# Moving the transposes of q and of the attention output off TensorE, in a linear attention followed by a sparse feed-forward layer

## The chip, the cores and the metric

The kernel runs on one core of a Trainium2 chip. The metric is the time of one execution on the device, in microseconds (us); the time before is the median of three runs.

## What is computed

The input x has 2 batches of 1024 tokens with 512 features, in float32. Two layers follow each other, each with a normalized input and a normalized, added output:

```
x = x + layernorm(attention(layernorm(x)))
x = x + layernorm(ffn(layernorm(x)))

attention: q = x Wq^T (16 heads of 128), k = x Wk^T, v = x Wv^T (4 heads of 128, each used by 4 heads of q)
           q, k = rope(q), rope(k);  qf, kf = elu(q) + 1, elu(k) + 1
           per token: state += kf v^T;  z += kf;  out = (qf . state) / (qf . z + 1e-6)
           attention = out Wo^T
ffn:       h = silu(x Wgate) * (x Wup)    (2048 wide)
           of every 4 neighbours in h keep the 2 of largest magnitude;  ffn = h Wdown
```

## The kernel before

**Tiles.** Attention runs in 16 steps: first all eight chunks of 128 tokens (both batches at once) with the first half of the heads, then the eight chunks again with the second half (`STEPS = 2 * NC`). In a step there are four blocks, one for each pair of batch and k/v head (`GROUPS`); a block has 128 tokens of four q heads that share one k head. The scan over tokens is done by chunk: scores of a block against its own chunk, masked to the causal half, plus the state of the chunks before.

**Products.** Each projection is a Strassen product in seven parts (`strassen`, L109): seven products of half-sized sums of inputs and weights, in the order 1, 2, 6, 5, 7, 4, 3, added into one PSUM bank `cb`, with copies to SBUF (`keep`, L120, ScalarE) in between and final sums on VectorE (L129, L139, L145). The sums of weights for the first half of the heads are built in SBUF by `sums`; those for the second half, and for the feed-forward layer, by a background generator `preparing`, of which one unit is a load on SP, four sums on GpSimd and seven stores on SP; it is advanced once for each block.

**q.** `q_products` (L634) gives four blocks; each goes through `features` (L584): the rotation (VectorE, L592 to L599; an addition on GpSimd, L600), ELU + 1 (two ScalarE activations, L602 and L603, and a VectorE operation, L604). The result `qf` has tokens on partitions. `q_transposed` (L663) turns it with four 128x128 TensorE transposes into PSUM (`transposed`, L528, L532), and ScalarE copies it to `qT` (L665), with head features on partitions and, for each head, 128 tokens in a row.

**Scores and numerators.** `scores` (L668) multiplies k's transposed block with all four heads of `qT`; VectorE masks the result into `am` (L679). `attend` (L684) takes for each head h the 128 tokens of `qT` and `am` as the stationary operand, against state and v, and VectorE divides by the denominator (L703 to L706). The quotient `o` has tokens on partitions, one head after the other.

**The output projection.** `o_transposed` (L733) turns `o` in the same way; the blocks are the inputs of `o_products` (L747), the fourth after subtractions (L741 to L745). A step's output projection runs in the next step.

**Order.** TensorE, GpSimd and SP follow the order in which the program is written (`manual_schedule`); VectorE and ScalarE are ordered by a planner, but for a short part at the start. SP issues nearly all transfers, and its issues wait in order. In step n the loop writes: `first(0)` (transposes of q block 1 and of the last step's output block 3), five of k/v's products for step n + 1, `second(0)` (numerators of block 0, scores of block 1), the rest of k/v, q's products for step n + 1 with block 1 in between, k's transposes, then the output products of step n - 1 around blocks 2 and 3. The last step interleaves the first gate products of the feed-forward layer.

**Buffers.** PSUM: three banks for products (`ps_mm`), two for transposes (`ps_tr`), one for scores, two for numerators. x has three buffers, `qf` three, `qT` two.

Of the kernel before, what the change touches and what calls it, by code (L numbers as in the profile page):

```python
# [15 lines left out]
P = 128  # L16
# [19 lines left out]
def kernel(  # L36
# [21 lines left out]

    ident = const.tile([P, P], F32, name="ident")
# [13 lines left out]
    eps = const.tile([P, 1], F32, name="eps")  # L73
    nc.gpsimd.memset(eps, LN_EPS)
# [12 lines left out]
    xf_dram = [dram.tile([P, 7, 2, P], F32, name=f"xf{c}") for c in range(NC)]  # L87
    y_dram = [dram.tile([P, B, DM], F32, name=f"y{c}") for c in range(NC)]
# [5 lines left out]
    def layernorm_scale(src, tag):  # L94

        st = small.tile([P, nc.vector.BN_STATS_DIM], F32, tag=f"st{tag}", name="st")
        nc.vector.bn_stats(st, src)
        mv = small.tile([P, nc.vector.BN_AGGR_DIM], F32, tag=f"mv{tag}", name="mv")
        nc.vector.bn_aggr(mv, st)
        sd = small.tile([P, 1], F32, tag=f"sd{tag}", name="sd")  # L100
        nc.scalar.activation(sd, mv[:, 1:2], AF.Sqrt, bias=eps)
        rs = small.tile([P, 1], F32, tag=f"rs{tag}", name="rs")
        nc.vector.reciprocal(rs, sd)
        return mv[:, 0:1], rs
# [4 lines left out]
    def strassen(pools, shape, product, c11, c12, c22, done):  # L109
# [24 lines left out]
        e = bank("ce")  # L134
# [4 lines left out]
        nc.vector.tensor_tensor(c22, s3, e, ALU.add)  # L139
# [5 lines left out]
        nc.vector.tensor_tensor(c12, s2, e, ALU.add)  # L145
# [42 lines left out]
    def ffn_input(xns, psum, tag, engine=None):  # L188
        xnT = pool["xs"].tile([P, NIC, 4 * P], F32, tag="fxnT", name="fxnT")
        for tt in range(4):  # L190
            pt = psum.tile([P, NIC, P], F32, tag=tag, name="psx")
            for j in range(NIC):
                nc.tensor.transpose(pt[:, j, :], xns[tt][:, j, :], ident)
            nc.scalar.copy(xnT[:, :, tt * P : (tt + 1) * P], pt)
        t = pool["xs"].tile([P, 3, 2, 256], F32, tag="fxt", name="fxt")
        return combinations(
            t,
            xnT[:, 0:2, 0:256],
            xnT[:, 0:2, 256:512],
            xnT[:, 2:4, 0:256],  # L200
            xnT[:, 2:4, 256:512],
            engine,
        )
# [110 lines left out]
    def down(hf):  # L314


        def product(bank, i, start):
# [3 lines left out]
            for jb in range(NJB):  # L321
                for j in range(2):
                    for k in range(2):
                        nc.tensor.matmul(  # L324
                            bank[:, j, :],
                            hf[jb][hi][:, k, j * P : (j + 1) * P],
                            w[:, jb, k, :],
                            start=(start and jb == 0 and j == 0 and k == 0),
                            stop=(jb == NJB - 1 and j == 1 and k == 1),
                            skip_group_check=True,  # L330
                        )
# [10 lines left out]
                lambda t: nc.scalar.copy(y[:, 0:2, 256:512], t),  # L342
            )
# [3 lines left out]
    def ffn_output(m, tt, xt_, y):  # L347
        b, c = place(m, tt)
        mean, rs = layernorm_scale(y, "y")
        yn = pool["ln"].tile([P, DM], F32, tag="ln", name="fyn")  # L350
        normalize(yn, y, mean, rs)
        nc.gpsimd.tensor_tensor(yn, xt_, yn, ALU.add)  # L352
# [22 lines left out]
    xp = left("a_x", 3)  # L375
# [4 lines left out]
    ps_mm = left("ps_mm", 3, space=PSUM)  # L380
    ps_tr = left("ps_tr", 2, space=PSUM)
# [30 lines left out]
    def sums(t, engine):  # L412
        a11, a12, a22, s2, s4, s3, s1 = (t[:, i] for i in range(7))
        for o, i0, i1, op in (
            (s1, s3, a22, ALU.add),
            (s3, a11, s3, ALU.subtract),
            (s2, s1, a11, ALU.subtract),
# [9 lines left out]
    xt = {0: load_x(0)}  # L427
# [3 lines left out]
    load_quarters(wq_sb, q_quarter, (nc.scalar, nc.sync))  # L431
    rope_sb = rawp.tile([P, NC, 3, HD // 2], F32, name="rope_sb", bufs=1)
    nc.scalar.dma_start(out=rope_sb, in_=rope.rearrange("(c p) t d -> p c t d", p=P))
    xt[1] = load_x(1)
    wo_sb = new_factors("wo", 4, 256)
    load_quarters(wo_sb, o_quarter, (nc.sync,))
    xt[2] = load_x(2)
# [96 lines left out]

    xf = {}
# [9 lines left out]
    def step_input(n, xns):  # L545

        t = ln.tile([P, 7, 2, P], F32, tag="xf", name="xf")
        xf[n] = t
        for b in range(B):
# [6 lines left out]
        nc.vector.tensor_tensor(t[:, 4], t[:, 2], t[:, 3], ALU.subtract)  # L556
        nc.vector.tensor_tensor(t[:, 5], t[:, 4], t[:, 0], ALU.subtract)
        nc.vector.tensor_tensor(t[:, 6], t[:, 1], t[:, 4], ALU.subtract)
        nc.sync.dma_start(out=xf_dram[n], in_=t)
# [24 lines left out]
    def features(src, c, dst):  # L584

        half = HD // 2
        cos = rope_sb[:, c, 0, :].unsqueeze(1).broadcast_to([P, 8, half])
        nsin = rope_sb[:, c, 1, :].unsqueeze(1).broadcast_to([P, 4, half])
        psin = rope_sb[:, c, 2, :].unsqueeze(1).broadcast_to([P, 4, half])
# [8 lines left out]
        nc.vector.tensor_tensor(r[:, :, 0:half], src[:, :, half:HD], nsin, ALU.mult)  # L598
        nc.vector.tensor_tensor(r[:, :, half:HD], src[:, :, 0:half], psin, ALU.mult)  # L599
# [8 lines left out]
    kf, kT, v1, qf = {}, {}, {}, {}  # L608
    GROUPS = ((0, 0), (1, 1), (0, 1), (1, 0))

    def kv_products(n):
        c = n % NC
# [13 lines left out]
        features(raw, c, f)  # L626
# [7 lines left out]
    def q_products(n):  # L634
        c = n % NC
        raw = [rawp.tile([P, REP, HD], F32, tag="raw", name="qraw", bufs=4) for _ in range(3)]

        def feature(i, src):
            f = qp.tile([P, REP, HD], F32, tag="qf", name="qf", bufs=3)
            features(src, c, f)  # L640
            qf[n, i] = f
# [19 lines left out]
    qT, am, o = {}, {}, {}  # L661

    def q_transposed(n, i):  # L663
        t = qp.tile([P, REP, P], F32, tag="qT", name="qT")
        nc.scalar.copy(t, transposed(qf.pop((n, i))))  # L665
        qT[n, i] = t

    def scores(n, i):  # L668
        b, j = GROUPS[i]
        sc = ps_sc.tile([P, REP, P], F32, tag="sc", name="sc")  # L670
        nc.tensor.matmul(  # L671
            sc.rearrange("p h t -> p (h t)"),
            kT[n][:, 2 * b + j, :],
            qT[n, i].rearrange("p h t -> p (h t)"),
# [3 lines left out]
        t = qp.tile([P, REP, P], F32, tag="am", name="am")  # L678
        nc.vector.tensor_tensor(  # L679
            t, sc, causal.unsqueeze(1).broadcast_to([P, REP, P]), ALU.mult  # L680
        )
        am[n, i] = t

    def attend(n, i):  # L684
# [8 lines left out]
        q, a = qT.pop((n, i)), am.pop((n, i))  # L693
        for h in range(REP):
            dst = nmv[:, h // 2, h % 2, :]
            if c > 0:
                nc.tensor.matmul(dst, q[:, h, :], state[b, j], start=True, stop=False)  # L697
            nc.tensor.matmul(dst, a[:, h, :], v, start=(c == 0), stop=True)  # L698
# [6 lines left out]
        t = qp.tile([P, REP, HD], F32, tag="o", name="o")  # L705
# [6 lines left out]
        o[n, i] = t  # L712
# [12 lines left out]
    later = []  # L725
# [6 lines left out]

    def o_transposed(n, i):  # L733

        t = transposed(o.pop((n, i)))
        if i < 3:
            place = (0, 2, 1)[i]
            nc.scalar.copy(factor(n, place, 1 if place == 1 else 2), t)
        else:
            t1, t2, t3, t4 = (factor(n, 3 + k, 1) for k in range(4))  # L740
            nc.vector.tensor_tensor(t1, t, of[n, 0], ALU.subtract)  # L741
            nc.vector.tensor_tensor(t2, of[n, 2], t1, ALU.subtract)
            t3_engine = nc.gpsimd if n + 1 < STEPS else nc.vector
            t3_engine.tensor_tensor(t3, t2, of[n, 0], ALU.subtract)
# [265 lines left out]
```

## Time and profile before

| | |
|---|---|
| median of 3 runs | 1395.71 us (1395.39 to 1396.8) |
| the profiled execution | 1395.51 us |
| its span, first to last instruction | 1393.8 us |
| TensorE busy / weight loads busy | 1335.9 / 1069.0 us |
| VectorE / ScalarE / GpSimd busy | 835.1 / 447.3 / 321.5 us |
| bytes moved by DMA | 197.48 MB, mean 142 GB/s |

A line of the profile's groups names line, engine, operation, output <- inputs, shapes and count, then busy time and the mean of one in nanoseconds. Busy times on TensorE overlap between neighbours, since matmuls are pipelined; the distance from start to start is what one holds of the engine. A wait line has waiter <- releaser, then total us, times, longest. L532 is line 532 of the kernel shown.

### The profile page before, as it was taken

How to read it: one execution, taken by the hardware profiler on the slowest of the kernel's cores; microseconds unless marked ns; L12 is line 12 of the kernel's file. 1: busy time of each engine (PE TensorE's matmuls, PEld its weight loads, DVE VectorE, ACT ScalarE, POOL GpSimd, SP SyncE). 2: the span in 40 equal slices, each digit the busy share in tenths (PEclk: the TensorE clock that was granted, in tenths of full speed). 3: DMA queues.
4: the chain of work that ended last, by engine and by line, in shares of the span. 5: the costliest groups of instructions: out<-in, count | busy, mean ns of one | idle time of the engine just before them, and what ended most of it. 6: DMA issues, size and time to landing. Idle time of an engine off the chain costs nothing. (4 is left out here: it accounts for less than half of the span.)

```text
span 1393.8 us, 17195 instructions
## 1 busy us (share of the span) xinstructions
PE 1335.9 (96%) x6384; PEld 1069.0 (77%) x6384; DVE 835.1 (60%) x1570; ACT 447.3 (32%) x797; POOL 321.5 (23%) x259
## 2 busy tenths in 40 slices
PE   4899999999999999999999999999999999999997
PEld 2567778777876787667678888888888888888886
DVE  5785766564556565656566439816772577526852
ACT  1543433433233324333342323214330333113210
POOL 0333322332333343444332110100000100110001
PEclk9999999999999999999999999999999999999999
DMA  6131345035841736233443455346544655355321
GB/s 245 42 125 52 105 162 186 28 97 178 274 140 64 242 113 215 82 108 123 153 144 129 128 213 152 116 165 217 152 128 152 222 153 154 117 201 152 91 79 73
DMA packets 109732, 197.48 MB, mean 142 GB/s; under 512 B 8272, under 2 KB 51280, under 8 KB 105552
## 3 DMA queue, kind: packets, MB, share of 16 engines
q1 hardware_dynamic: 107520, 194.02, 43.1%
q10 hardware_dynamic: 2128, 2.36, 0.5%
q8 instruction: 51, 0.84, 0.2%
q14 instruction: 33, 0.27, 0.1%
HBM read 145.23 MB, written 51.12 MB: 141 GB/s over the span
## 5 line engine op out<-in xcount | busy, mean ns | idle before, releaser
L120 ACT COPY u<-cb 128x512 f32<-128x512 f32 (+1 forms) x252 | 126.1, 500 | 474.7 <-PE cb L218 183.1
L600 POOL TENSOR_TENSOR u<-u,r 128x512 f32<-128x512 f32 x80 | 101.8, 1273 | 300.9 <-DVE r L599 190.1
L570 PE MATMUL cb<-wq,xf 128*128 128x512 f32 x256 | 121.3, 596 | 7.0 <-ACT u L120 7.0
L755 PE MATMUL cb<-wo,of 128*128 128x256 f32 x512 | 121.2, 379 | 0.5 <-ACT u L120 0.5
L218 PE MATMUL cb<-fxt,wgu 128*128 128x256 f32 x512 | 117.8, 381 | 1.0 <-ACT u L120 1.0
L218 PE MATMUL cb<-fxnT,wgu 128*128 128x256 f32 x512 | 116.9, 379 | 0.0
L755 PEld LDWEIGHTS cb<-wo,of 128*128 128x128 f32 x512 | 95.9, 190 | 26.3 <-issue 11.9
L218 PEld LDWEIGHTS cb<-fxt,wgu 128*128 128x128 f32 x512 | 96.6, 190 | 16.4 <-ACT u L120 3.6
L218 PEld LDWEIGHTS cb<-fxnT,wgu 128*128 128x128 f32 x512 | 97.1, 190 | 13.8 <-issue 0.5
L604 DVE SCALAR_TENSOR_TENSOR qf<-u,r 128x512 f32<-128x512 f32 x64 | 65.4, 1021 | 66.3 <-ACT r L603 58.4
L168 POOL TENSOR_TENSOR h<-h 128x512 f32<-128x512 f32 x16 | 23.5, 1467 | 331.1 <-DVE ht L165 331.1
L602 ACT ACTIVATE r<-u 128x512 f32<-128x512 f32 x80 | 50.4, 631 | 153.9 <-POOL u L600 153.9
L139 DVE TENSOR_TENSOR y<-u,ce 128x256 f32<-128x256 f32 (+1 forms) x20 | 9.5, 474 | 146.8 <-ACT u L120 146.8
L698 PE MATMUL nm<-v,am 128*128 128x129 f32 x512 | 96.0, 277 | 1.5 <-DVE am L679 1.5
L570 PEld LDWEIGHTS cb<-wq,xf 128*128 128x128 f32 x256 | 46.6, 190 | 55.9 <-issue 40.7
L697 PE MATMUL nm<-state,qT 128*128 128x129 f32 x448 | 86.6, 275 | 0.0
L698 PEld LDWEIGHTS nm<-v,am 128*128 128x128 f32 x512 | 76.8, 194 | 3.4 <-issue 3.3
L697 PEld LDWEIGHTS nm<-state,qT 128*128 128x128 f32 x448 | 71.0, 191 | 7.7 <-issue 6.2
L570 PE MATMUL cb<-wkv,xf 128*128 128x256 f32 x256 | 67.8, 388 | 1.9 <-DVE xf L556 1.4
L671 PE MATMUL sc<-qT,kT 128*128 128x512 f32 x128 | 66.1, 598 | 0.0
L324 PE MATMUL cb<-wd,h 128*128 128x256 f32 x256 | 58.3, 381 | 4.0 <-DVE h L306 3.9
L755 PE MATMUL ce<-wo,of 128*128 128x256 f32 x256 | 60.5, 379 | 0.0
(151 smaller groups left out, 2571.6 us busy)
## 6 DMA issues: line engine op xcount, KB each, us to landing
wgu<-gs SPq DMA_DIRECT2D x112, 256.0 KB, 2.7
wgu<-us SPq DMA_DIRECT2D x112, 256.0 KB, 2.7
wd<-d_dram SPq DMA_DIRECT2D x28, 1024.0 KB, 4.8
xf<-xf SPq DMA_DIRECT2D x16, 896.0 KB, 5.1
x<-in_x_dram SPq DMA_DIRECT2D x16, 512.0 KB, 5.9
gs<-wraw SPq DMA_DIRECT2D x28, 256.0 KB, 3.5
us<-wraw SPq DMA_DIRECT2D x28, 256.0 KB, 3.5
d_dram<-wraw SPq DMA_DIRECT2D x28, 256.0 KB, 2.8
```

The costliest lines, as they stand in the source:

```text
L120: nc.scalar.copy(t, b)
L168: (engine or nc.gpsimd).tensor_tensor(b12, b22, b12, ALU.subtract)
L218: nc.tensor.matmul(bank[:, j, :], w[:, k, j, :], xf[xi][:, k, :], start=(start and j == 0 and k == 0), stop=(j == 1 and k == 1), skip_grou ...
L324: nc.tensor.matmul(bank[:, j, :], hf[jb][hi][:, k, j * P : (j + 1) * P], w[:, jb, k, :], start=(start and jb == 0 and j == 0 and k == 0), ...
L570: nc.tensor.matmul(bank.rearrange("p h d -> p (h d)"), x_[:, xi, k, :], w[:, wi, k, :], start=(start and k == 0), stop=(k == 1), skip_grou ...
L600: nc.gpsimd.tensor_tensor(u, u, r, ALU.add)
L602: nc.scalar.activation(r, u, AF.Relu, scale=-1.0)
L604: nc.vector.scalar_tensor_tensor(dst, u, 0.0, r, ALU.max, ALU.add)
L671: nc.tensor.matmul(sc.rearrange("p h t -> p (h t)"), kT[n][:, 2 * b + j, :], qT[n, i].rearrange("p h t -> p (h t)"), start=True, stop=True,)
L697: nc.tensor.matmul(dst, q[:, h, :], state[b, j], start=True, stop=False)
L698: nc.tensor.matmul(dst, a[:, h, :], v, start=(c == 0), stop=True)
L755: nc.tensor.matmul(bank.rearrange("p h d -> p (h d)"), of[n, xi][:, k, :], w[:, wi, k, :], start=(start and k == 0), stop=(k == 3), skip_g ...
```

## The change

In words:

- q features: VectorE transposes 32x32 blocks inside the tile (`turned`), SP stores the result to HBM in one transfer of 256 KB (`q_store`), and four transfers of 64 KB bring it back with the blocks in their places (`q_load`). In the loaded tile the free axis is four groups of 32 tokens, each with all four heads; numerators are made for 32 tokens of four heads at a time, and the mask is taken in that order.
- The output blocks take the same way (`o_store`, `o_load`) straight into the inputs of the output products; the subtractions stand together in `o_sums`. The last step keeps TensorE's transposes.
- Order in a step: q's products come first, k/v's behind numerators of block 0; k's transposes stand between output products. Loads of the second half's weights are spread over a step.
- The rope table is loaded for each step; rotation's two half-sized products become one. x has two buffers, `qf` one, `qT` four; product banks are four, transpose banks one.
- Start: x in two halves on two queues, weight sums on GpSimd, ScalarE's root used once ahead. End: the last down product has two banks, so that half of it is finished ahead; statistics of two halves are merged, the last addition is on VectorE.

```diff
+    def turned(src):
+        t = qp.tile([P, 4, 4, 32], F32, tag="blocks", name="blocks", bufs=4)
+        nc.vector.transpose(
+            out=t.rearrange("p b i r -> p i b r"),
+            in_=src.rearrange("p i (b d) -> p i b d", d=32),
+        )
+        return t
+
+    def store_blocks(t, to):
+        nc.sync.dma_start(out=to, in_=t.rearrange("p b i r -> p (b i r)"))
+
+    def load_blocks(t, of_):
+        for b in range(4):
+            nc.sync.dma_start(
+                out=t[b * 32 : (b + 1) * 32],
+                in_=of_.rearrange("(u d) (b e) -> b d u e", u=4, b=4)[b],
+            )
...
         def feature(i, src):
-            f = qp.tile([P, REP, HD], F32, tag="qf", name="qf", bufs=3)
-            features(src, c, f)
-            qf[n, i] = f
+            f = qp.tile([P, REP, HD], F32, tag="qf", name="qf", bufs=1)
+            features(src, n, f)
+            q_blocks[n, i] = turned(f)
...
-    def q_transposed(n, i):
-        t = qp.tile([P, REP, P], F32, tag="qT", name="qT")
-        nc.scalar.copy(t, transposed(qf.pop((n, i))))
-        qT[n, i] = t
+    def q_store(n, i):
+        store_blocks(q_blocks.pop((n, i)), qb_dram[n % 2][i])
+
+    def q_load(n, i):
+        t = qp.tile([P, 4, P], F32, tag="qT", name="qT", bufs=4)
+        load_blocks(t, qb_dram[n % 2][i])
+        qT[n, i] = t
...
-        for h in range(REP):
-            dst = nmv[:, h // 2, h % 2, :]
+        for u in range(4):
+            dst = nmv[:, u // 2, u % 2, :]
             if c > 0:
-                nc.tensor.matmul(dst, q[:, h, :], state[b, j], start=True, stop=False)
-            nc.tensor.matmul(dst, a[:, h, :], v, start=(c == 0), stop=True)
+                nc.tensor.matmul(dst, q[:, u, :], state[b, j], start=True, stop=False)
+            nc.tensor.matmul(dst, a[:, u, :], v, start=(c == 0), stop=True)
...
+        if n + 1 < STEPS:
+            blocks[n, i] = turned(t)
+        else:
+            o[n, i] = t
...
-        nc.vector.tensor_tensor(r[:, :, 0:half], src[:, :, half:HD], nsin, ALU.mult)
-        nc.vector.tensor_tensor(r[:, :, half:HD], src[:, :, 0:half], psin, ALU.mult)
+        nc.vector.tensor_tensor(
+            r.rearrange("p h (t d) -> p h t d", t=2),
+            src.rearrange("p h (t d) -> p h t d", t=2)[:, :, ::-1, :],
+            sin,
+            ALU.mult,
+        )
...
-    ps_mm = left("ps_mm", 3, space=PSUM)
-    ps_tr = left("ps_tr", 2, space=PSUM)
+    ps_mm = left("ps_mm", 4, space=PSUM)
+    ps_tr = left("ps_tr", 1, space=PSUM)
```

The order of a step in the changed kernel, for a step in the middle (one line for each call; `run(g, k)` makes k of the seven products of g):

```
first(0):  o_store(n-1, 3); q_load(n, 3); o_load(n-1, 3); preparing
run(q, 5)
second(0): q_store(n+1, 0); attend(n, 0); scores(n, 1)
first(1):  o_store(n, 0); q_load(n+1, 0); o_load(n, 0); preparing
run(q, 1); run(kv, 1); finish(q); run(kv, 4)
second(1): q_store(n+1, 1); q_store(n+1, 2); attend(n, 1); scores(n, 2)
first(2):  q_store(n+1, 3); o_store(n, 1); q_load(n+1, 1); o_load(n, 1); load_rope(n+2); preparing
finish(kv); o_sums(n-1); input of step n+2; run(o, 3)
second(2): attend(n, 2); scores(n, 3)
first(3):  o_store(n, 2); q_load(n+1, 2); o_load(n, 2); preparing
run(o, 1); k_transposed(n+1); run(o, 1)
second(3): attend(n, 3); scores(n+1, 0)
finish(o)
```

## The prediction

> **What bounds the kernel now.** I read the page's engine table and slices first, then the stretches of one step, then the timeline of TensorE inside a step, the table of waits, and last the timelines of start and end. The engine table and TensorE's slices:
>
> ```profile
> PE 1335.9 (96%) x6384; PEld 1069.0 (77%) x6384; DVE 835.1 (60%) x1570; ACT 447.3 (32%) x797; POOL 321.5 (23%) x259
> ...
> PE   4899999999999999999999999999999999999997
> ```
>
> TensorE is full in all slices but the first two and the last. The scores of block 0 mark the steps; the stretch table over one step from there to there has length, then busy time of PE, PEld, DVE, ACT, POOL, then clock, DMA share, GB/s:
>
> ```profile
> 551.00:597.46 46.46, 45.90 (x231) 34.48 (x230) 28.25 (x60) 17.49 (x33) 18.47 (x15) 1.00 0.39 130
> 597.46:645.82 48.36, 46.12 (x231) 34.39 (x230) 31.16 (x60) 17.52 (x33) 21.54 (x17) 1.00 0.36 131
> ```
>
> A step is TensorE's 46 us, and 2 us more where it waits; VectorE has 15 us to spare, the DMA engines 60%. So work taken off TensorE comes off the time until something else is late. What a transpose holds is not its busy time. TensorE's timeline:
>
> ```profile
> 568.54 0.60 PE L532 MATMUL pst<-ident,qf 128*128 128x128 f32 x4
> ...
> 568.98 0.60 PE L532 MATMUL pst<-ident,o 128*128 128x128 f32 x4
> ...
> 569.41 1.88 PE L570 MATMUL cb<-wq,xf 128*128 128x512 f32 x4
> ```
>
> The second column is 0.60, but the next group starts after 0.44 and 0.43. Four transposes cost **0.435 us**. The waits of TensorE that the change could touch, in total, times, longest:
>
> ```profile
> PE pst L532 <- DVE x L107: 16.9, 2, 8.7
> PE cb L570 <- ACT u L120: 7.5, 6, 2.0
> PE pst L532 <- ACT qT L665: 5.8, 20, 0.9
> ```
>
> The first is the start, where TensorE has no other work. The second is a copy that waits in ScalarE's order behind a feature map; the third is the evacuation of transposes.
>
> **Transposes off TensorE.** 64 of q and 60 of the output's 64 go (the last step keeps four): 124 x 0.435 = **53.9 us**. The busy column would give 38.5 + 38.5 x 60/64 = 74.6, which is too much, since neighbours overlap. With them goes the third wait, **5.8 us**. ScalarE loses 64 copies at 579 ns and 45 at 584, 63 us in all, but isn't the bound: nothing counted.
>
> **VectorE's new work.** 124 transposes of 128x512 f32. No row shows one. Below, the nearest by form (one input, SBUF to SBUF, same size) is the normalization of fxn at 580 ns; above, the fused last operation of a feature, 1021 ns, whose mean includes waits beside GpSimd. The Trainium skill's "VectorE: DVE Perf Modes", section "The three transpose paths", speaks against the change: it prices a 128x128 bf16 transpose at 311 ns on VectorE, 32x32 blocks only, and its rules send a 128x128 transpose to TensorE where PSUM will do. By it (an estimate: 311 plus 384 more columns at the 0.96 GHz it gives) one of ours is 711 ns; against TensorE's measured 435 that is a loss if the two engines' time were worth the same. It isn't here: one has no idle time and the other 35%. I take 0.70 us, nearest to the 671 ns row of the x normalization. Eight a step are 5.6 us. Each feature's two rotated products (415 + 416 ns) become one of full size (about 690), 0.14 x 5 = 0.7 us less. VectorE goes from 28.6 us (mean over 13 steps) to **33.5** of a step of about 43, 78%. Cover is thus thinner: at 1.02 it is 36 us. The first of the subtractions for the output (L741, 687) now reads SBUF, at 690 to 951 like its neighbours; inside that rounding.
>
> **What is late next.** The matmuls with the numerators wait for the masked scores. After the reorder the shortest distance is for block 3: one output product (1.72), k's transposes (0.44), another product (1.72), 3.9 us, against 5.2 before. In it VectorE does the former block's den, reciprocal, o, the new transpose and the state (0.15 + 0.18 + 0.69 + 0.70 + 0.28 = 2.0, the first 0.9 of it before the scores end) and the mask, 0.68: done 1.8 us after the scores if VectorE is free, 2 us of slack. One operation that is held beside GpSimd (the trace has 1.75) eats that. I charge 0.5 us a step, 14 steps, **+7 us**; bounds 0 and 35 (2.5 a step).
>
> **q first, k later.** k's products move behind q's first five and block 0. Their chain (last sum at 565.60, kf done at 572.5) takes 7 us; k's transposes now stand three output products, one block and another product behind, 9.7 us. Block 0's scores follow 4 us later against one copy at 575 ns. Nothing on the path. If k is 3 us late, TensorE waits those 3.
>
> **The way through HBM.** q block 0: feature chain 5 to 8.5 us (568.81 to 577.31 is the longest I saw), transpose 0.7, store, load. A 256 KB store lands in 2.0 us (the output's row), a 256 KB load in 2.7 (weights of gate). The loads are four of 64 KB. "DMA: Bandwidth & Descriptors", section "Rules for kernel authors", says that under 64 KB one pays mostly overhead[...]. Taken one behind the other, 32 loads a step would be 64 us, longer than the step, and the change a loss. The trace has the 112 gate loads at 320 ns on SP each, landing at 2.7, so transfers overlap and the issue counts: four loads 1.3 us. From q product 2 to the loaded block: 8.5 + 0.7 + 2.0 + 1.3 + 2.7 = 15 us, and it is wanted at the end of the step, 35 us on. The output goes out at one step and is summed in the middle of the next: over 15 us to spare for its last block. **0 us**, as long as SP keeps up.
>
> **SP's order** is fixed by hand, so a store that waits for VectorE holds all behind it: q's and o's loads, the preparation of weights, x. A step had about 15 issues (prepared weights 10.7, four others); it gets 8 stores, 32 loads and a rope table, 56. The 15 take about 9 us (store pieces of 512 bytes 0.84, of weights 0.44, loads 0.7); 41 x 0.32 = 13; waits for VectorE, by my laying out of the order, 7. Together 29 of 43 us. GpSimd's preparation waits for loads that now stand behind those, some 4 us later within a quarter of a step of slack (10 us).
>
> **DMA engines.** 4.2 MB a step more, at the 287 GB/s of a stretch in which only stores from 512-byte pieces run, 14.5 us, on 0.39 x 46.5 = 18: 76% of 43. Not the bound on average.
>
> **Start and end.** VectorE's timeline at the start:
>
> ```profile
> 8.51 0.69 DVE L97 BATCH_NORM_STATS2 st<-x 128x6 f32<-128x512 f32 x1
> 15.68 0.69 DVE L97 BATCH_NORM_STATS2 st<-x 128x6 f32<-128x512 f32 x1 [6.48 <-DMA x<-in_x_dram]
> ```
>
> Batch 1 of the first tile stands behind the statistics of the second tile's x. That load is issued after the first input now, so this 6.5 us can go; the root's table (1.28) is loaded ahead, and x in halves on two queues saves about 1. On GpSimd the first two of the kv sums take 2.5 us, beside normalization; wq's four, 2.6 each as for wo, end some 12 us after kv starts, before product 3 wants the last. From 0 (another operation waits for the same load) to 11; I take **9**. At the end, the last sum, two statistics, normalization twice and GpSimd's 1.26 stand between TensorE's end at 1384.4 and the last issue at 1390.7. Half-sized sums (0.42 for 0.69), statistics of one half only and VectorE's add (0.69) leave 3.2 of 6.2: **3 us**.
>
> **Sum.** 1393.8 - 53.9 - 5.8 - 9 - 3 + 7 = 1329.1 span; the profiled execution has 1.7 around its span, 1330.8, and stands 0.2 under the median shown: **1331**.
>
> **Rivals.**
> *VectorE's order becomes the bound* (22%): its transposes at 1 us or its waits beside GpSimd make TensorE wait 2.5 us in each of 14 steps, 35 instead of 7: **1359**. For it: 78% load in fixed order and the 2.00 us wait already there. Against: 1.8 us of work in 3.9 at the tightest place.
> *The start and the waits go better* (20%): no new waits, 11 us at the start, and the 7.5 us of waits for copies vanish with ScalarE's 63 us: 1331 - 7 - 2 - 7.5 = **1315**.
> *SP can't issue in time, slower than before* (8%): the loads back up as the 512-byte stores do, 0.84 a piece instead of 0.32. 56 issues and the waits: 9 + 41 x 0.84 + 7 = 50 us a step against 46.7 now. The step is then SP's: 14 x 3.7 = 52 us, less the 12 of start and end: **1436**. It loses from 47.6 us a step on, an issue of 0.77. Against: pieces of a 64 KB load are a quarter of a 256 KB store's.
> The forecast itself has the remaining 50%.
>
> **From these to the range.** Faster 0.91, the remainder slower save 0.01 for no change; 0.2% either way, 2.8 us, is about what this measurement can tell. The range runs from 1307 (the better case, with 8 us for the order of waits I can't see) to 1367 (the VectorE case, same margin); SP's case and a little at each end stay outside.
>
> **What would show it.** Right: TensorE's 128x128 groups from qf and o gone but for the last four, its busy time near 1260; steps of 42.5 to 43.5 us; VectorE transposes near 0.70; the first kv product near 10 us; TensorE's waits few and under a microsecond. Wrong: waits of the numerators for masked scores (L679) or of scores for loaded q in each step, SP's loads at over 0.7 us, transposes over 1 us, or the kv product at 18 us still.

## The result, and the profile after

The changed kernel takes 1433.4 us (median; 1429.74 to 1440.19) against 1395.72 us for the kernel before, run beside it: a ratio of 1.0274, 95% interval 1.0232 to 1.0316. It is slower by 38 us where 65 us less were forecast. The profiled execution took 1429.74 us, its span is 1428.0.

The page's engine table and TensorE's slices with the granted clock, after:

```profile
PE 1313.1 (92%) x5888; PEld 1033.9 (72%) x5888; DVE 892.0 (62%) x1612; ACT 402.1 (28%) x698; POOL 336.0 (24%) x265
...
PE   5889989899789878898898999999999999999997
...
PEclk9889999999989999999999999999999999999999
```

TensorE lost its 496 transposing matmuls (6384 to 5888), but its busy time fell by 22.8 us only, from 1335.9 to 1313.1, and what it is not busy rose from 57.9 us to 114.9. The slices, nines from the third on before, have eights and sevens up to slice 22, near the end of attention. Two stretches from one step's first scores to the next's, same columns as before:

```profile
580.28:627.20 46.92, 44.35 (x199) 32.49 (x198) 32.90 (x63) 13.89 (x26) 19.14 (x15) 0.96 0.62 196
627.20:678.20 51.00, 45.80 (x199) 32.84 (x198) 34.92 (x63) 14.11 (x26) 21.83 (x17) 0.93 0.71 234
```

With 32 matmuls less, TensorE is busy nearly as long as before (44.35 and 45.80 us against 45.90 and 46.12), at a clock of 0.96 and 0.93, and stands 2.6 and 5.2 us besides. The mean of the 14 steps is 49.6 us ((781.33 - 86.62) / 14, from the scores of step 1 to those of step 15), against 46.7 before. The new operations in the groups, and the transfers (count, size, median us from issue to landing):

```profile
L581 DVE STREAM_TRANSPOSE blocks<-qf 128x512 f32<-128x512 f32 x64 | 44.9, 702 | 0.3
...
L581 DVE STREAM_TRANSPOSE blocks<-o 128x512 f32<-128x512 f32 x60 | 41.4, 689 | 0.0
```

```profile
qT<-qb SPq DMA_DIRECT2D x256, 64.0 KB, 2.3
of<-ob SPq DMA_DIRECT2D x240, 64.0 KB, 2.0
```

A transpose costs what it was priced at, 0.70 us. The issue of a 64 KB load holds SP for 0.47 us in the mean of the 14 steps (median 0.43), where 0.32 was forecast. The waits of TensorE, after (total, times, longest):

```profile
PE cb L635 <- ACT u L133: 27.2, 23, 5.5
PE ce L635 <- DVE r L662: 14.3, 10, 2.8
...
PE pst L568 <- DVE kf L672: 8.7, 7, 4.3
PE cb L635 <- DMA xf<-xf: 8.3, 2, 7.3
PE cb L838 <- DVE of L825: 8.3, 4, 3.2
PE cb L635 <- DMA wq<-wq_dram: 7.9, 1, 7.9
```

None of these six was above 8 us before. A product waits for ScalarE's copy of the bank that it adds to, for VectorE's read of a bank (`r` is the rotation of q's third block, read from PSUM), for k's features, for the sums of loaded output blocks, and for loads. The waits that the prediction looked for, numerators for masked scores, are not among them.

What such a wait costs is more than its length. TensorE's timeline after, and three stretches behind waits (length, busy times, then clock, DMA share, GB/s):

```profile
395.69 3.75 PE L635 MATMUL cb<-wq,xf 128*128 128x512 f32 x4 [7.88 <-DMA wq<-wq_dram]
...
403.09 1.88 PE L635 MATMUL cb<-wq,xf 128*128 128x512 f32 x4
```

```profile
396.00:400.00 4.00, 4.00 (x8) 1.93 (x8) 0.00 (x0) 0.52 (x1) 0.00 (x0) 0.50 1.03 377
...
210.00:214.00 4.00, 4.00 (x11) 3.18 (x12) 4.00 (x9) 0.84 (x2) 0.00 (x0) 0.50 0.17 66
...
556.80:560.00 3.20, 3.20 (x11) 2.84 (x12) 2.80 (x4) 1.53 (x4) 1.26 (x1) 0.50 0.67 188
```

The four matmuls behind 7.88 us of waiting take 3.75 us at a clock of 0.50, the same four 1.88 us some 7 us later. The second stretch follows a wait of 5.48 us, the third two shorter ones, of 2.78 and 1.00 us within 5 us.

### The profile page after: what moved, and what is told of

It is laid out like the page before. It is cut to its first block, busy times and chain, and to the rows that moved or that the text cites. A ratio compares the mean times of both kernels' runs of the same rounds, so it can differ in the third digit from the quotient of the medians.

```text
span 1428.0 us, 17352 instructions
## 1 busy us (share of the span) xinstructions
PE 1313.1 (92%) x5888; PEld 1033.9 (72%) x5888; DVE 892.0 (62%) x1612; ACT 402.1 (28%) x698; POOL 336.0 (24%) x265
## 4 chain that ended last, share of the span: by engine, by line
PE 64%; DVE 16%; DMA 5%; ACT 5%; issue 4%; POOL 3%; SPq 3%; DVEq 0%; ACTq 0%; POOLq 0%
PE cb L237 15%; PE ce L237 8%; PE cb L346 6%; PE cb L838 6%; PE cb L635 5%; PE ca L237 4%; PE ce L346 4%; POOL u L668 3%; PE nm L766 3%; DVE blocks L581 2%; PE nm L765 2%; PE ce L838 2%; DVE r L662 2%; PE sc L740 2%; PE ce L635 2%
## 5 line engine op out<-in xcount | busy, mean ns | idle before, releaser
L668 POOL TENSOR_TENSOR u<-u,r 128x512 f32<-128x512 f32 x80 | 106.0, 1326 | 308.8 <-DVE r L662 240.4
L635 PE MATMUL cb<-wq,xf 128*128 128x512 f32 x256 | 128.5, 626 | 23.5 <-DMA xf<-xf 8.3
L838 PE MATMUL cb<-wo,of 128*128 128x256 f32 x512 | 124.9, 388 | 9.6 <-DVE of L825 8.3
L635 PEld LDWEIGHTS cb<-wq,xf 128*128 128x128 f32 x256 | 49.6, 199 | 83.8 <-issue 65.9
L766 PE MATMUL nm<-v,am 128*128 128x129 f32 x512 | 101.0, 289 | 2.1 <-ACT state L787 2.1
L765 PE MATMUL nm<-state,qT 128*128 128x129 f32 x448 | 92.1, 289 | 0.0
L635 PE MATMUL cb<-wkv,xf 128*128 128x256 f32 x256 | 73.4, 413 | 19.9 <-ACT u L133 19.9
L672 DVE SCALAR_TENSOR_TENSOR qf<-u,r 128x512 f32<-128x512 f32 x64 | 58.2, 910 | 48.4 <-ACT r L671 43.4
L766 PEld LDWEIGHTS nm<-v,am 128*128 128x128 f32 x512 | 82.4, 206 | 3.8 <-ACT state L787 2.5
L635 PEld LDWEIGHTS cb<-wkv,xf 128*128 128x128 f32 x256 | 50.4, 203 | 47.1 <-ACT u L133 28.0
L765 PEld LDWEIGHTS nm<-state,qT 128*128 128x128 f32 x448 | 77.5, 206 | 9.2 <-issue 6.8
```

The costliest lines, as they stand in the source:

```text
L635: nc.tensor.matmul(bank.rearrange("p h d -> p (h d)"), x_[:, xi, k, :], w[:, wi, k, :], start=(start and k == 0), stop=(k == 1), skip_grou ...
L668: nc.gpsimd.tensor_tensor(u, u, r, ALU.add)
L672: nc.vector.scalar_tensor_tensor(dst, u, 0.0, r, ALU.max, ALU.add)
L765: nc.tensor.matmul(dst, q[:, u, :], state[b, j], start=True, stop=False)
L766: nc.tensor.matmul(dst, a[:, u, :], v, start=(c == 0), stop=True)
L838: nc.tensor.matmul(bank.rearrange("p h d -> p (h d)"), of[n, xi][:, k, :], w[:, wi, k, :], start=(start and k == 0), stop=(k == 3), skip_g ...
```

## The experiments

Four questions: what the relief of TensorE is worth for nothing, what VectorE's transposes and the way through HBM cost each, whether the new order or the banks cost anything, and what start and end gave. All times are medians; ratios are to the kernel before in the same runs, with 95% intervals. The planner orders VectorE and ScalarE anew for each kernel, so differences of a few us between kernels of different code are not read as effects of one edit.

### TensorE relieved for nothing

**Before, without the transposes.**

```diff
-        nc.scalar.copy(t, transposed(qf.pop((n, i))))
+        nc.scalar.copy(t, qf.pop((n, i)))
...
-        t = transposed(o.pop((n, i)))
+        t = o.pop((n, i))
```

> The kernel before, order and buffers untouched, with the TensorE transposes of q and of the output left out and nothing in their place: ScalarE copies the untransposed tiles where it copied the transposed ones. TensorE has 56 us less work, VectorE, GpSimd, SP and the DMA engines exactly as before. It is the most that taking these transposes off TensorE can give in that order. BOUND (as the prediction had it: TensorE's work is the time, and what the change loses is lost to what it adds): 1336 to 1346. CHAIN (in the middle of a step the chain product, ScalarE copy, VectorE, GpSimd's addition, two activations, VectorE is as long as TensorE's work, and a product of the output waits for the PSUM bank that q's third block is still read from): well under half of it, 1370 to 1400, and the granted clock falls with the waits.

1374.67 us, 0.9838 (0.9823 to 0.9853). TensorE's busy time falls by 53.5 us, to 1282.4, so the price of a transpose (53.5 / 128 = 0.42 us) was right. The time falls by 22. This kernel's waits:

```profile
PE cb L755 <- ACT u L120: 18.3, 14, 1.7
...
PE ca L755 <- DVE r L599: 11.3, 11, 1.6
PE cb L570 <- ACT u L120: 10.6, 11, 2.0
```

40 us of waits stand where these three had 8. None of them is above 2 us, and the clock stays at 0.994. What they name is a second chain that was nearly as long as TensorE's work: product, ScalarE's copy out of the bank, VectorE's rotation, GpSimd's addition, ScalarE's two activations, VectorE; each of these engines in a fixed order. The relief was not quite for nothing: VectorE's last operation of a feature takes 1.27 us here in the mean, against 1.02 before. In the run with three and two banks below it takes 1.01, and the time is about the same, so this does not explain the missing 32 us.

**The changed order without both, four and three product banks.** Features and quotients go straight into the tiles that the matmuls read; nothing is transposed, stored or loaded.

```diff
-            f = qp.tile([P, REP, HD], F32, tag="qf", name="qf", bufs=1)
-            features(src, n, f)
-            q_blocks[n, i] = turned(f)
+            qT[n, i] = qp.tile([P, 4, P], F32, tag="qT", name="qT", bufs=8)
+            features(src, n, qT[n, i])
```

> The changed kernel's order, start and end with neither VectorE's block transposes nor the stores and loads: features and quotients are written straight into the tiles that the matmuls read (blocks are untransposed, so the output is not the reference's). ADDITIVE: transposes and the way through HBM each are paid in full, the 20 us without the one come on top of the 27 without the other: 1383-1391. SHARED: both make the same matmuls late and only the later of them counts: 1397-1405. If the new order were harmless, the time would be that of the old order with transposes left out, 1374.

> The changed kernel's order, start and end without VectorE's block transposes and without stores and loads (the output is not the reference's), with the PSUM banks of before, three and two. Beside the same without the transposes in the old order and the old banks (1374.7) only the order differs, and the start and end, which gave 1 us. If the order itself costs nothing: 1371-1377. If the order costs what its run with four banks stands above, or more: 1380-1400.

1380.35 us with the change's banks, 0.9881 (0.9866 to 0.9896), and 1372.54 with those of before, 0.9823 (0.9807 to 0.984). The second against 1374.67 differs in order, start and end: the new order by itself costs nothing. Relief for nothing is worth 22 us in the old order, and 15 to 23 in the new.

**The bank.** More than a quarter of the 40 us of waits is for VectorE's reading of a product bank (`r`, 11.3). Four product banks, one for transposes, in the order of before, without transposes and with them:

```diff
-    ps_mm = left("ps_mm", 3, space=PSUM)
-    ps_tr = left("ps_tr", 2, space=PSUM)
+    ps_mm = left("ps_mm", 4, space=PSUM)
+    ps_tr = left("ps_tr", 1, space=PSUM)
```

> The order and the work of before, the TensorE transposes of q and of the output left out (ScalarE copies the tiles untransposed, so the output is not the reference's), and the eight PSUM banks shared out as in the change: four for the products, one for the remaining transposes, instead of three and two. BANK: a third of what is still lost without the transposes is TensorE waiting for the bank that VectorE still reads for q's third block; with a fourth bank the wait of the output's second factor for VectorE's r (11.3 us with three) falls under 3 us and the time is 1355-1366. CHAIN: the copies in ScalarE's order and VectorE's order hold TensorE somewhere else a moment later; that wait shrinks, another grows, and the time stays at 1368-1378.

> Before with four banks for products and one for transposes, nothing else. BANK: before has about 8 us of waits for copies and 6 for evacuations of transposes; the fourth bank takes at most 3 of the first, the single transposing bank adds 0.3-0.6 us to every second group of transposes (some 190 groups): 1400-1450. If the evacuations are quick enough to be hidden by the products between, 1393-1397.

> The changed kernel with the PSUM banks of before, three for the products and two for transposes, nothing else. BANK: the fourth bank keeps TensorE from waiting for VectorE's read of q's third block; with three the change is slower still, 1440-1460, and the wait of a product for VectorE's r (14.3 us) grows past 25. NONE: only k's and the inputs' transposes are left for the second bank and one product more for the fourth, within 4 us of 1433. HARM: the single transposing bank is part of what the change lost, as it was of the old order's (159 us there): 1415-1428.

1398.78 us without the transposes, 0.9999 (0.9985 to 1.0013): slower than with three banks, in each of its 20 runs (1390.96 to 1402.33). The wait for `r` has gone, as foreseen, and the wait for ScalarE's copies has grown from 18.3 us:

```profile
PE cb L755 <- ACT u L120: 31.5, 15, 3.3
```

The clock falls to 0.982: of the 27 us by which the profiled execution is longer, TensorE's busy time has 17 (1282.4 to 1299.4), which neither forecast counted, and both missed the time. So a fourth product bank, bought with a transposing bank, does not take the lost time back. Before with its transposes and four banks takes 1555.6 us, 1.1145 (1.1128 to 1.1162), far beyond both guesses, on waits for the evacuation of the single transposing bank (111.7 us) and on 50 us more of TensorE's busy time:

```profile
PE pst L532 <- ACT qT L665: 68.2, 62, 3.0
PE pst L532 <- ACT of L738: 43.5, 20, 2.7
```

The other way round, the changed kernel with three and two banks, takes 1433.69 us, 1.0266 (1.0245 to 1.0288): no difference. Its wait for `r` is 41.0 us instead of 14.3, that for copies 10.7 instead of 27.2. The wait changes its name, and the time stays.

### VectorE's transposes and the way through HBM

**Without the one, and without the other.** In the first, untransposed blocks are stored and loaded; in the second, VectorE transposes 32x32 blocks straight into the tiles of use, and blocks are not put in their places. Neither computes the reference.

```diff
-            q_blocks[n, i] = turned(f)
+            q_blocks[n, i] = f
```

```diff
-        store_blocks(q_blocks.pop((n, i)), qb_dram[n % 2][i])
...
-        load_blocks(t, qb_dram[n % 2][i])
```

> The changed kernel without VectorE's 124 transposes: features and quotients are written into the tiles that are stored, so that what comes back is not transposed. VectorE has 5.6 us less in a step, all else is as it was. PLACE: most waits stay: 1400 to 1420. LOAD: waits of k/v's products go: 1340 to 1370. PATH: nothing, 1420 to 1435.

> The changed kernel with VectorE writing its transposes straight into the tiles in which they are used: no store and no load of q and the output (the 32x32 blocks are turned, but not exchanged among each other). 40 issues and 4.2 MB a step less, VectorE as it was. PLACE: small, 1400 to 1425 (the waits for late loads go, the others stay). LOAD: as PLACE. PATH: 1340 to 1370.

1413.0 us without VectorE's transposes, 1.0104 (1.008 to 1.0128); 1406.18 without HBM, 1.0043 (1.0021 to 1.0065). With the run that has neither they make a square: from 1380.35, transposes add 25.8 us and HBM 32.7; from the other side, to 1433.4, they add 20.4 and 27.2. Both are paid, though VectorE is idle 38% of the time after the change, and TensorE waits for a loaded q block only once (1.3 us). How the 53 us divide is less certain than these figures look: of the 20 runs without HBM eight lie near 1395.5 us and twelve at 1406 to 1411, and from the lower group the transposes would have 15 and HBM 38. What parts the groups is open. The kernels without HBM also have more buffers for `qT`, eight for four. What the transposes do is seen between the runs without HBM, without transposes and then with them:

```profile
PE cb L633 <- ACT u L133: 43.3, 23, 5.0
...
PE ce L633 <- DVE r L660: 7.5, 8, 1.5
```

```profile
PE cb L633 <- ACT u L133: 34.1, 25, 5.0
PE ce L633 <- DVE r L660: 25.8, 12, 2.8
```

The products wait 18 us more for the bank of q's third block, 9 less for copies, and TensorE's busy time grows from 1296.3 to 1309.0. The changed kernel shows how, in VectorE's timeline and TensorE's:

```profile
551.90 0.68 DVE L656 TENSOR_TENSOR u<-cb,rope 128x512 f32<-128x512 f32 x1
552.50 0.70 DVE L581 STREAM_TRANSPOSE blocks<-qf 128x512 f32<-128x512 f32 x1
553.12 0.66 DVE L581 STREAM_TRANSPOSE blocks<-o 128x512 f32<-128x512 f32 x1
553.72 0.64 DVE L662 TENSOR_TENSOR r<-cb,rope 128x512 f32<-128x512 f32 x1
```

```profile
554.51 1.23 PE L635 MATMUL ce<-wkv,xf 128*128 128x256 f32 x4 [2.78 <-DVE r L662]
```

Two transposes stand between the two operations that read bank `cb`, and the product that needs the bank starts when the second has read it. No run put these reads ahead of the transposes in VectorE's order.

**The traffic without its waits.** The last kernel, and all of the stores and loads at their places on SP, but from a constant tile and into a tile that nobody reads (still not the reference).

```diff
     def q_store(n, i):
-        pass
+        store_blocks(idle_in, qb_dram[n % 2][i])
...
     def q_load(n, i):
-        pass
+        idle_load(qb_dram[(n + 1) % 2][i])
```

> The changed kernel with VectorE's block transposes written straight to where they are used, and every store and load of the way through HBM issued at its place on SP, but from a tile that is constant and into a tile that nobody reads (blocks are untransposed in the large, so the output is not the reference's): the same issues and bytes, without the waits for VectorE's blocks, for the stores to land, and without anything that waits for the loads. WAITS: the 27 us of the way through HBM come from SP standing for VectorE (163.8 us) and for landings (64.4 us), which makes inputs and weights late: 1403-1412. ISSUES: they come from 40 more issues a step and from 4.2 MB a step more in the DMA engines, which delay the other loads: 1422-1435.

1399.91 us, 1.0019 (1.0007 to 1.0031). Beside the run without HBM (1406.18; its lower group 1395.5) the same 40 issues and 4.2 MB a step cost nothing, or 4.4 us at most; 33 us are in the waits. SP's own, in the changed kernel:

```profile
SPq L588 <- DVE blocks L581: 163.8, 47, 14.5
...
SPq L593 <- DMA ob<-blocks: 64.4, 25, 6.8
```

Over 15 steps that is 10.9 us a step for VectorE and 4.3 for landings, against 7 forecast. Issues hold SP for 28.3 us of a step (mean of 14), against 22 forecast: together 43.5 of 49.6 us, and as much as the whole step of 42.5 to 43.5 that was forecast. All that stands behind a waiting store is late: the change's SP timeline shows an input's load, and TensorE's shows who wanted it at 523.8:

```profile
513.12 0.32 SPq L588 DMA_DIRECT2D ob<-blocks  x1
514.57 2.76 SPq L593 DMA_DIRECT2D qT<-qb  x4
517.38 1.85 SPq L593 DMA_DIRECT2D of<-ob  x4
...
519.80 2.37 SPq L505 DMA_DIRECT2D us<-wraw  x4
522.22 2.67 SPq L493 DMA_DIRECT2D gs<-wraw  x3
524.93 0.87 SPq L628 DMA_DIRECT2D xf<-xf  x1
```

```profile
531.11 3.78 PE L635 MATMUL cb<-wq,xf 128*128 128x512 f32 x4 [7.34 <-DMA xf<-xf]
```

TensorE's waits for `xf` and `wq`, 16.2 us in the changed kernel, don't occur in this run at all. Nor does the wait for the summed output blocks (8.3), but that one is no late load: VectorE, which makes the sums, stands for no load ahead of them. It is at work, with the sums behind a transpose (the product waits 3.19 us, until 267.84):

```profile
264.73 0.70 DVE L581 STREAM_TRANSPOSE blocks<-o 128x512 f32<-128x512 f32 x1
265.35 1.40 DVE L824 TENSOR_TENSOR of<-of 128x512 f32<-128x512 f32 x1
```

Late loads reach the features by another way, GpSimd, which waits for the weights to prepare and has rotation's additions behind that:

```profile
118.15 1.51 POOL L497 TENSOR_TENSOR wraw<-wraw 128x512 f32<-128x512 f32 x1 [7.71 <-DMA wkv_dram<-wraw]
...
121.31 1.72 POOL L668 TENSOR_TENSOR u<-u,r 128x512 f32<-128x512 f32 x1
```

VectorE had this addition's operand ready at 117.93. Six of the 80 additions start over 2 us late after the change, the latest by 6.5; none does before or without HBM, and one (2.7) with the unwaited traffic. Which of these waits weighs how much was not tried one by one; nor was the traffic with the waits of loads alone or of stores alone.

### The order

**The changed order with TensorE's transposes.** Everything of the change but where the transposes are done; ScalarE copies them to SBUF in the new layout. **k/v products first.** The change with the old place of q's chain. **The same, with the sums of the output blocks earlier.**

```diff
+        pt = transposed(q_blocks.pop((n, i))).rearrange("p h (u t) -> p h u t", t=32)
+        nc.scalar.copy(t.rearrange("p u (h t) -> p h u t", t=32), pt)
```

```diff
             first(0)
+            run(kvp, 5)
...
+            second(0)
+            finish(kvp)
...
                 run(qpr, 2)
```

```diff
             run(wkv_loads, 3)
+            if n > 0:
+                o_sums(n - 1)
             first(1)
```

> The changed kernel with the transposes of q and of the output back on TensorE (and ScalarE's copies); its order of a step, start, end, weight loads and banks stay. Three theories. PLACE: k/v's seven products, 0.86 us each, now stand among the four feature maps of q, and the ScalarE copy that each waits for stands in ScalarE's order behind activations that wait for VectorE and GpSimd; the new order alone makes the waits, so TensorE gets 54 us of work back on top of them: 1450 to 1480. LOAD: VectorE's 5.6 us of transposes a step in that stretch make it late: the waits go, 1375 to 1395. PATH: SP's fixed order with 41 more issues a step brings inputs, weights and prepared weights late: the waits go as well, 1375 to 1395.

> The changed kernel with k/v's products first in a step and q's behind them, as before the change; the transposes stay on VectorE and go through HBM, the stores and loads of q moved with q's products. PLACE: waits of k/v's products go: 1330 to 1360. LOAD: the same work of VectorE in a step, late elsewhere: 1400 to 1430. PATH: same issues on SP: 1400 to 1430, but for the wait for the second half's weights of q (7.9 us and a slow clock after it), which has its slack again.

> As the run with k/v's products first, but the subtractions for the output projection stand in VectorE's order ahead of q's last features (after q's second product) and not behind them, where that run waited 5 to 8 us a step for them. PLACE (what is behind the burst of q's features waits for it, whichever product it is): those waits go, 1340 to 1380. LOAD: VectorE is as loaded as before and something else waits: 1410 to 1440. PATH: late loads stay: 1410 to 1440.

1452.34 us, 1.0398 (1.037 to 1.0427); 1450.17, 1.0372 (1.0352 to 1.0392); 1448.87, 1.0382 (1.0366 to 1.0397). The first agrees with the theory that the new place of q's products is what costs; the second was to gain 70 us or more by that theory, and lost 17. The theory falls as it stands. In the first, TensorE waits 44.1 us for ScalarE's copies of product banks: the new order without ScalarE's 124 copies of transposes is harmless (1372.54; 1380.35 with this run's banks), with them it isn't, and what that says of the two together was not taken further. Its single transposing bank is not what it waits for (3.0 us for both copies of transposes). In the second the waits move to the output products (for ScalarE's `r`, 38.4 us in 8 times), in the third back to copies (23.6) and to a late input (22.8).

### VectorE's load, part by part

**Output alone through VectorE and HBM**, in the order of before. **The rotation's addition moved from GpSimd to VectorE** in that kernel, in the change, and in the kernel before.

```diff
-        o[n, i] = t
+        if n + 1 < STEPS:
+            blocks[n, i] = turned(t)
+        else:
+            o[n, i] = t
```

```diff
-        nc.gpsimd.tensor_tensor(u, u, r, ALU.add)
+        nc.vector.tensor_tensor(u, u, r, ALU.add)
```

> The kernel before in its own order, with only the output's transposes on VectorE and through HBM (60 of 64 blocks; stores and loads where its transposes stood, the subtractions after q's second product); q stays on TensorE, its copy lays out 32 tokens of four heads. TensorE has 26 us less, VectorE 2.8 us a step more, SP 20 issues a step more. PLACE: no product is moved into the burst of q's features, so the gain comes: 1368 to 1380. LOAD: half of the transposes already cost waits: 1385 to 1400. PATH: half of the issues, and the subtractions wait for late loads: 1385 to 1400.

> The run with only the output's transposes moved (1426), with the addition of each feature map on VectorE and not on GpSimd: the chain of a block is shorter by GpSimd's 1.27 us and its place behind the prepared weights; VectorE has 5 x 0.7 = 3.5 us more a step, 10 without its waits beside GpSimd. CHAIN: the waits of the output's products for the bank go, 1375 to 1400. LOAD: VectorE's work is what is late: 1430 to 1450. PATH: 1420 to 1430.

> The changed kernel (1433) with the addition of each feature map on VectorE and not on GpSimd. CHAIN: 1385 to 1410, since the keep copies no longer stand behind activations that wait for GpSimd. LOAD: VectorE at 36 us of a step, 1440 to 1460. PATH: 1425 to 1435.

> The kernel before with the addition of each feature map on VectorE and not on GpSimd, nothing else: the control of the two runs beside it. CHAIN: the waits of 2 us in steps 10, 12 and 13 and little more can go: 1386 to 1394. LOAD: 1396 to 1410.

Output alone: 1426.47 us, 1.022 (1.0205 to 1.0235); every theory had 1368 to 1400. The addition there: 1437.53, 1.0294 (1.0277 to 1.0311); in the change: 1419.36, 1.0162 (1.0138 to 1.0185); in the kernel before: 1408.76, 1.0085 (1.007 to 1.01). The timeline of the run with the output alone, VectorE and TensorE:

```profile
603.29 0.69 DVE L626 SCALAR_TENSOR_TENSOR qf<-u,r 128x512 f32<-128x512 f32 x1 [1.16 <-ACT r L625]
603.90 0.70 DVE L540 STREAM_TRANSPOSE blocks<-o 128x512 f32<-128x512 f32 x1
604.53 0.65 DVE L614 TENSOR_TENSOR u<-cb,rope_sb 128x512 f32<-128x512 f32 x1
...
605.43 0.41 DVE L621 TENSOR_TENSOR r<-cb,rope_sb 128x256 f32<-128x256 f32 x1
```

```profile
605.94 2.98 PE L791 MATMUL ca<-wo,of 128*128 128x256 f32 x8 [4.38 <-issue]
```

VectorE waits 1.16 us for a feature, makes it, transposes `o`, and only then reads bank `cb`; a product starts 0.1 us after the last read, 4.38 us late. The profile names no releaser for it; that it is this read is inferred from the times, and from the same product's waits for `r` in the run without transposes. The transpose is 0.70 us of these. In the kernel before, 47.7 us more on VectorE (835.1 to 882.8) cost 12 us while it still idles 37%. In the change the same move gains 14, where GpSimd's additions could start late behind waits for loads; that this is the reason is an argument and not shown. VectorE's load alone is not the cause, then; which of load and chain counts differs with the order around.

### Start and end

Both parts alone on the kernel before, then the end alone.

```diff
-            finish(sums(wkv_sb, nc.vector))
+            finish(sums(wkv_sb, nc.gpsimd))
...
-        y = down(hf)
+        end = m + 1 == NM
+        y = down(hf, end)
```

> The kernel before with the changed start (x in halves on two queues, second x and Wo loaded later, weight sums on GpSimd, root's table ahead) and the changed end (last down product in two banks, merged statistics, additions on VectorE), nothing else. The sum put them at 9 and 3: 1384 by all theories; if the start gives nothing, 1393; if its later loads cost, over 1396.

> Before with the end alone of the change (half-sized last sums, statistics by halves, the last additions on VectorE). The end's own saving, by the timeline of the run with start and end (TensorE's end to the end of the span 7.4 us against 9.4), is 2 us: 1393-1394.5. If it is lost in the same way as there, 1395.3-1396.

1395.79 us, 0.9991 (0.9983 to 0.9999); the end alone 1394.74, 0.9989 (0.9982 to 0.9997). TensorE's timeline with both parts:

```profile
12.68 1.91 PE L591 MATMUL cb<-wkv,xf 128*128 128x256 f32 x4
...
33.49 1.31 PE L553 MATMUL pst<-ident,x 128*128 128x128 f32 x8 [1.16 <-DVE x L114]
...
49.11 2.08 PE L591 MATMUL cb<-wkv,xf 128*128 128x256 f32 x4 [3.48 <-ACT u L128]
...
58.78 1.02 PE L692 MATMUL sc<-qT,kT 128*128 128x512 f32 x2
```

The first product starts at 12.68 instead of 18.85 us; the first scores at 58.78, where they were at 58.42. The six microseconds are given back in waits, of which the lines show two, for the second input and for a copy. Of the end, 1.5 us remain.

## Why the prediction was wrong

Its sum, with measured terms: 1395.7; everything removed, with new order, start and end, 15 us (forecast 53.9 + 5.8 + 9 + 3 = 71.7); VectorE's transposes +26 (forecast +7 for waits); the way through HBM +27 (forecast 0): 1433.4. The gap of 102 us is 56 of relief not had, 19 and 27. By the other way round the square it is 56, 13 (transposes +20) and 33 (HBM +33).

- **Prices: right but for one.** 0.435 us for four transposes on TensorE (0.42), 0.70 us on VectorE (0.702, 0.689), VectorE's step of 33.5 us (33.1, mean of 14), loads that overlap. Their issue was priced too low, at 0.32 us for 0.47 measured. Still the row was the better guide than 64 us of loads one behind the other: 496 loads of 64 KB cost 4 us at most by themselves.
- **The failing step: "work taken off TensorE comes off the time until something else is late", with "What is late next".** The prediction read 96% busy and few waits as one bound and looked for one successor. But few waits mean only that nothing else was *longer*. The runs with the relief for nothing show the slack: of 59.7 us to be removed (53.9 + 5.8), 15 to 23 came off the time, and the rest stood as waits in the chain through ScalarE, VectorE, GpSimd and back. The 2.00 us wait for a copy "in ScalarE's order behind a feature map", shown in the prediction's own waits, was a sign of it. The numerators' masked scores, at which the waits were charged, had slack: the profile after the change has no wait of TensorE for them.
- **VectorE's cover.** "78% of a step" is a mean. What the transposes are added to is the stretch between a product and the release of its bank, where VectorE has no 15 us to spare. The rival in which VectorE's order becomes the bound had the mechanism, at the wrong wait; the 20 to 26 us measured lie between its 35 and the forecast's 7.
- **The way through HBM, "0 us, as long as SP keeps up".** q's and o's blocks were in time. What was late was the rest of SP's queue. The sum of 29 of 43 us was 43.5 of 49.6 (28.3 of issues for 22, 15.2 of waits for 7), and a wait in an ordered queue delays what stands behind it even where the sum fits. The prediction named this for GpSimd's preparation, and gave it 10 us of slack, but costed nothing for it, for inputs or for weights. The rival that ended slower, SP unable to issue in time, named 1436, near the 1433.4 by chance: an issue of a load took 0.47 us, under its deciding 0.77, and the issues unwaited cost 4 us at most.
- **The clock.** The prediction used full speed throughout. The Trainium skill's "TensorE: Matmul & The Clock Gate", Part 1, puts the array at half rate after an idle window of some 3.4 us; the stretches at 0.50 behind waits of 7.88 and 5.48 us agree, and the one behind 2.78 and 1.00 us shows that several shorter waits do it too. By the run without transposes TensorE's work at near full clock is 1282.4 + 4 x 0.42 = 1284.1 us; it was busy 1313.1. So some 29 us are the clock's, as much as half of the added idle time (57.0). The granted clock agrees: the changed kernel has 14 half-speed stretches with 64.1 us of TensorE's work in them, half of it lost, 32 us, against 3 before. The longer span is thus 51.8 us of work less, 29 more for the clock and 57 more of waits: 34.2.
- **Start, 9 us, and end, 3:** 1 together. The start was costed to the first product, not to the first scores, which kept their place.

## What to carry to other kernels

An engine at 96% with short waits can have a second chain right beneath it: before pricing what replaces its work, leave the work out for nothing, since here 54 us of it were worth 22. In an engine or queue that works in order, look at what stands behind an added wait rather than at its spare time: the traffic alone cost 4 us at most, the waits 33. Price waits of TensorE with the half-speed stretch that can follow them: here 57 us of added idle time brought 29 of slower work.

## What the runs showed of the hardware

496 loads of 64 KB with 124 stores, in the middle of other traffic, land in 2.0 and 2.3 us (medians) in the changed kernel; issued without waits they land in 2.3 and 3.5 us and hardly slow it (1399.91 with, 1406.18 or 1395.5 without). 32x32 transposes of a 128x512 float32 tile on VectorE take 0.69 to 0.70 us, what the division of that size by the denominators takes (L706 before, 0.69). One PSUM bank for transposes and four for products, instead of two and three, cost 159 us in a kernel whose profile showed 5.8 us of waits for the evacuation of transposes. In the kernel before, VectorE's last operation of a feature (L604) takes 0.69 us in each of 52 cases in which no operation of GpSimd overlaps it, and 1.47 in the mean, 1.75 at most, in the 28 in which one does.
